# A graph attention layer: the edge and mask products of two neighbouring pairs issued together on the two halves of the array, and a new order of the stages in a round

## The chip, the cores and the metric

The kernel runs on one core of one Trainium2 chip. The metric is device time in microseconds (us), lower is better. Five engines matter: TensorE (PE, with its weight loads shown as PEld) multiplies matrices, VectorE (DVE) and ScalarE (ACT) do elementwise work and read the products out of PSUM, GpSimd (POOL) issues the gathers, and SyncE (SP) issues the other DMAs. Each engine takes its instructions in the order in which the program wrote them and waits for the others through semaphores.

## What is computed

A graph with 12,500 nodes and 400,000 edges, sorted by destination. After a layer norm and a ReLU, a GATv2 attention layer with 8 heads of 16 channels gathers over the edges, and a feed-forward block follows. The part that fills the time is the loop over edges:

```python
x_l = (x @ W_l).reshape(n, H, C)
x_r = (x @ W_r).reshape(n, H, C)
e = (ea @ W_e).reshape(-1, H, C)
m = jax.nn.leaky_relu(x_l[src] + x_r[dst] + e, NEG_SLOPE)
alpha = jnp.einsum('ehc,hc->eh', m, att)
amax = jax.ops.segment_max(alpha, dst, num_segments=n)
expa = jnp.exp(alpha - amax[dst])
denom = jax.ops.segment_sum(expa, dst, num_segments=n)
a = expa / (denom[dst] + 1e-16)
out = jax.ops.segment_sum(x_l[src] * a[:, :, None], dst, num_segments=n)
...
h = x + _gatv2(_ln(x, ln1_g, ln1_b), edge_index, edge_attr, ...)
ff = jax.nn.gelu(_ln(h, ln2_g, ln2_b) @ W1 + b1, approximate=False) @ W2 + b2
return h + ff
```

## The kernel before

A first part normalises the nodes, writes the left features to `xl_dram` and prepares the indices. Then `window_edges` works through the edges. 512 edges are a **pair** (two units of 256 edges, four tiles of 128), so there are 782 pairs, `c = 0 .. 781`. All rows are float32 except the masks.

One pair passes through these steps. Each is a function of `window_edges`, with the engine that does it:

- `gather` (POOL, L912): four indirect DMAs bring the source rows of the four tiles into `xs`, four rounds ahead. `windows` (SP, L926 to L945) brings edge attributes (`ea`), relative destinations (`dl`) and a 32-row window of right features (`zw`).
- `place` (DVE, L953): writes the 0/1 matrix of the destinations into the rows of `ea` below the 32 attribute rows, so that one product with 64 rows (32 attributes and 32 window nodes) adds the edge term and the right feature. For even pairs it also writes the mask `ne` of this pair and the next one (L959).
- `combine` (PE): four transposes of `xs` open the PSUM bank `z` (L966), and the 64-row product of `zw` and `ea` closes it (L970). A float32 product is two PE instructions in the trace. Even pairs keep their 64 rows on partitions 0 to 63 (`half`), odd pairs on 64 to 127.
- `slope` (ACT, L984) and `bend` (DVE, L989): 0.2 z, and the maximum with z, which is the leaky ReLU `m`.
- `apart` (PE, L977): a bfloat16 product of 64 rows opens the bank `ab` with a huge number for edges that do not belong to a node of the window. It uses `other`, the half of the partitions that the pair's own `zw` and `ea` do not use. `score` (PE, L994) adds the negative attention scores.
- `lowest` (DVE, L1000): the minimum over the edges of a unit, into `rec`. `weigh` (ACT, L1011, two instructions): the exponentials `p`.
- `turn` (PE, L1019): four transposes of `p` into `pt_ps`. `keep_turned` (ACT, L1024) copies them to `pt`.
- `collect` (PE, L1033): eight products add the weighted source rows into `acc`. `own_heads` (DVE, L1042 and L1048) keeps each head's own part, in `rec`, and `put` (SP, L1059) stores the record.

PSUM has four rings of two banks each: `z`, `ab`, `pt_ps` and `acc`. The work on finished groups of nodes (the `f_` functions: 25 groups of four tiles), on right features (`xr_steps`) and on some late left features (`raw_steps`) takes banks from the same rings, and is written after the stages of a round; `f_out` takes a bank of `ab`.

The order is written by hand. In round `r`, a table of stages is gone through from top to bottom, and an entry `(late, f)` does `f(r - late)`. So an engine's own order within a round is the order of the table, and `late` says by how many rounds a step follows `combine` of the same pair. Before the change a round on PE is: transposes and 64-row product of pair r, mask product of pair r-2, transposes of p of pair r-4, sums of pair r-6, scores of pair r-2. On DVE it is: own heads of r-7, lowest of r-3, bend of r-1, place of r+1. On ACT: copy of r-5, slope of r-1, exponentials of r-3.

Of the kernel before, what the change touches and what calls it, by code (L numbers as in the profile page):

```python
# [13 lines left out]
F32 = mybir.dt.float32  # L14
# [4 lines left out]
OP = mybir.AluOpType  # L19
# [3 lines left out]
P = 128  # L23
H = 8
C = P // H
DE = 32
# [811 lines left out]
def window_edges(  # L838
# [9 lines left out]
    nc = tc.nc  # L848
    SP = mybir.EngineType.SP
    KP = UP * KU  # L850
    EPR = UP * U
    LATE = 6
# [4 lines left out]
    n_pr = -(-NE // KP)  # L857
    pairs = [{} for _ in range(n_pr)]
# [7 lines left out]
    def edges_of(c):  # L866
        return [len(t) * P for t in tiles_of(c)]

    with ExitStack() as es:
# [4 lines left out]
        ps2 = es.enter_context(tc.tile_pool(name="e_ps2", bufs=2, space=PSUM))  # L874
# [74 lines left out]
        def place(c):  # L949

            d = pairs[c]
            rs = slice(d["half"].start + DE, d["half"].stop)
            nc.vector.tensor_scalar(  # L953
                d["ea"][rs].rearrange("p (a b) -> p a b", b=OW),
                d["dl"][rs].rearrange("p (a b) -> p a b", b=OS)[:, :, 0:OW],
                nid[rs], None, op0=OP.is_equal,
            )
            if c % 2 == 0:
                nc.vector.tensor_scalar(d["ne"][0 : P - DE], d["dl"][0 : P - DE, 0:EPR], nid[0 : P - DE], None, op0=OP.is_equal)  # L959

        def combine(c):

            d, e = pairs[c], sum(edges_of(c))
            z = ps2.tile([P, EPR], F32, name="z")
            for j in range(e // P):
                nc.tensor.matmul(  # L966
                    z[:, j * P : (j + 1) * P], d["xs"][:, j, 0:P], ident, start=(j == 0), stop=False, is_transpose=True
                )
            rs = d["half"]
            nc.tensor.matmul(z[:, :e], d["zw"][rs], d["ea"][rs, :e], start=False, stop=True)  # L970
            d["z"] = z

        def apart(c):
            d, e = pairs[c], sum(edges_of(c))
            d["ab"] = ps2.tile([P, EPR], F32, name="ab")
            rs = d["other"]
            nc.tensor.matmul(  # L977
                d["ab"][:, :e], farw.rearrange("p n h -> p (n h)")[rs], d["ne"][rs, :e], start=True, stop=False
            )

        def slope(c):
            d, e = pairs[c], sum(edges_of(c))
# [118 lines left out]
        def bank_of(d, name, ring="acc"):  # L1101
            d[name] = ps2.tile([P, EPR], F32, name=ring)
            return d[name]
# [99 lines left out]

        def f_out(d):
            n = d["n"]
            d["sum"] = bank_of(d, "sum", "ab")[:, 0 : n * P]
            part_out(d, 0, d["sum"])
            o = tiles("o", d, "f_e").rearrange("p t f -> p (t f)")
            part_out(d, 1, o)
            nc.vector.tensor_add(d["sum"], d["sum"], o)  # L1210
            d["o2"] = tiles("o2", d, "f_a").rearrange("p t f -> p (t f)")
            part_out(d, 2, d["o2"])
# [114 lines left out]
        def f_put(d):  # L1327
            nc.sync.dma_start(out_t[:, d["ts"], :], d["out"])

        stages = (  # L1330
            (-AHEAD, gather),
            (LATE + 1, own_heads),
            (5, keep_turned),
            (0, combine),
            (2, apart),
            (4, turn),
            (LATE, collect),
            (2, score),
            (3, lowest),
            (1, slope),  # L1340
            (1, bend),
            (3, weigh),
            (-1, place),
        )
        late_stages = (
            (-WAHEAD, windows),
# [111 lines left out]
        with tc.manual_schedule():  # L1458
            for r in range(-AHEAD, max(last_round, groups[-1]["round"] + 18)):
                in_round(r, early, groups[:-2])  # L1460
                for late, f in stages:
                    c = r - late
                    if 0 <= c < n_pr:
                        f(c)
                for late, f in sum_stages:
                    i, off = divmod(r - late, SUM_STEP)
# [9 lines left out]
                for late, f in late_stages:  # L1476
                    c = r - late
# [356 lines left out]
```

## Time and profile before

| | us |
|---|---|
| median of 3 runs (4754.81 to 4765.8) | 4760.2 |
| the profiled execution, its own time | 4798.77 |
| its span, first to last instruction | 4796.9 |
| PE busy in the span | 3841.3 (80%) |
| DVE busy | 2973.2 (62%) |
| POOL busy | 2965.3 (62%) |
| ACT busy | 2171.5 (45%) |
| mean granted PE clock | 0.897 of full |

Busy times are sums over one execution. Groups of instructions carry the line of the program, the names of what they write and read, and their shape; `64*128` behind a PE instruction is the part of the array that it uses, 64 rows by 128 columns. In a timeline, the first number is the start in us from the start of the span, the second the time that the merged instructions cover, and the bracket the idle time of the engine before them with what ended it. Ends of PE instructions are modelled, so their starts are the safer numbers. A wait that the trace ends with "remote" or "issue" has no releaser that it can name.

### The profile page before, as it was taken

The page shows a single profiled execution, that of the slowest core. Times are in us where ns is not written, and L with a number is a line of the kernel's source. Part 1 is how long each engine was busy: PE and PEld are TensorE (multiplying, and loading weights), DVE is VectorE, ACT ScalarE, POOL GpSimd, SP SyncE. Part 2 cuts the span into 40 slices and gives each one's busy share as a digit, 9 for nine tenths or more (in the row PEclk, how much of TensorE's full clock was granted, in tenths as well). Part 3 has the DMA queues.
Part 4 walks back from the last instruction along what each step waited for, and adds up shares of the span by engine and source line. Part 5 has one row for each costly group of instructions (what it writes and reads, how often), then busy time and mean ns, then how long its engine had stood idle before and what let it go on. Part 6 is the DMA issues. An engine that isn't in the chain of part 4 may idle for free.

```text
span 4796.9 us, 63161 instructions
## 1 busy us (share of the span) xinstructions
PE 3841.3 (80%) x18434; PEld 2388.1 (50%) x18435; DVE 2973.2 (62%) x6282; ACT 2171.5 (45%) x4746; POOL 2965.3 (62%) x3146
## 2 busy tenths in 40 slices
PE   2468888888888888887888888888888888888887
PEld 1335555555455555555555555555555555555554
DVE  3646676676666566566666566666666656656656
ACT  3624344344444445445444444444444454444444
POOL 6456666666666666666666666666666666666662
PEclk9679899898999999998999998899899999899898
DMA  6546666555544444444444444444444444444432
GB/s 156 173 112 149 156 158 150 138 133 132 130 99 95 92 94 96 87 85 89 93 90 92 96 94 92 84 95 82 93 97 91 92 89 87 92 87 83 94 79 66
DMA packets 625309, 502.69 MB, mean 105 GB/s; under 512 B 320174, under 2 KB 522013, under 8 KB 624717
## 3 DMA queue, kind: packets, MB, share of 16 engines
q1 hardware_dynamic: 524381, 281.11, 25.2%
q0 software_dynamic: 100000, 217.32, 21.5%
q8 instruction: 152, 2.49, 0.2%
q14 instruction: 200, 1.64, 0.1%
q10 hardware_dynamic: 576, 0.13, 0.0%
HBM read 432.27 MB, written 65.83 MB: 104 GB/s over the span
## 4 chain that ended last, share of the span: by engine, by line
PE 61%; DVE 12%; issue 11%; another core or an unknown queue 8%; ACT 2%; DMA 1%; POOL 1%; SPq 0%; DVEq 0%; ACTq 0%; POOLq 0%
PE acc L1033 15%; PE ab L994 13%; PE z L970 13%; PE pt_ps L1019 9%; PE z L966 7%; DVE rec L1000 2%; DVE ea L953 2%; DVE m L989 2%; DVE own L1042 2%; PE acc L1283 1%; PE acc L1308 1%; POOL xs L912 1%; ACT p L1011 1%; DVE ne L959 0%
## 5 line engine op out<-in xcount | busy, mean ns | idle before, releaser
L912 POOL DMA_INDIRECT xs<-xl_dram,src_sb x3009 | 2847.0, 946 | 1694.9 <-issue 787.9
L1011 ACT ACTIVATE p<-ab,rec 128x256 f32<-128x256 f32 x1563 | 656.0, 471 | 1179.5 <-DVE rec L1000 622.5
L1033 PE MATMUL acc<-xs,pt 128*128 128x136 f32 x6250 | 1017.3, 308 | 183.6 <-issue 131.3
L1042 DVE TENSOR_TENSOR own<-acc,diag 128x272 f32<-128x272 f32 x782 | 341.3, 436 | 1297.3 <-remote 517.6
L1033 PEld LDWEIGHTS acc<-xs,pt 128*128 128x128 f32 x6250 | 907.9, 214 | 213.1 <-issue 156.3
L970 PE MATMUL z<-ea,zw 64*128 64x512 f32 x1564 | 939.4, 681 | 37.6 <-issue 14.8
L1024 ACT COPY pt<-pt_ps 128x512 f32<-128x512 f32 x782 | 456.1, 583 | 1089.0 <-remote 463.9
L994 PE MATMUL ab<-m,negrep 128*128 128x512 f32 x1564 | 902.7, 659 | 29.8 <-issue 28.5
L966 PEld LDWEIGHTS z<-ident,xs 128*128 128x128 f32 x3125 | 401.6, 151 | 716.5 <-issue 346.8
L966 PE MATMUL z<-ident,xs 128*128 128x128 f32 x3125 | 519.5, 290 | 294.2 <-issue 86.5
L1019 PEld LDWEIGHTS pt_ps<-ident,p 128*128 128x128 f32 x3125 | 358.1, 150 | 729.1 <-issue 684.0
L1019 PE MATMUL pt_ps<-ident,p 128*128 128x128 f32 x3125 | 563.8, 306 | 87.7 <-issue 72.1
L953 DVE TENSOR_SCALAR ea<-dl,nid 32x516 f32<-32x516 bf16 x782 | 582.0, 744 | 29.4 <-DMA dl<-dc_dram 4.2
L989 DVE TENSOR_TENSOR m<-z,zs 128x512 f32<-128x512 f32 x782 | 532.9, 681 | 96.7 <-issue 45.1
L1000 DVE TENSOR_REDUCE rec<-ab 128x2 f32<-128x512 f32 x781 | 533.5, 683 | 76.7 <-remote 35.6
L984 ACT ACTIVATE zs<-z 128x512 f32<-128x512 f32 x782 | 475.4, 608 | 40.4 <-DMA ea<-in_ea_t 19.7
L977 PE MATMUL ab<-ne,farw 64*128 64x512 bf16 x782 | 319.2, 408 | 98.6 <-ACT p L1011 65.4
L1048 DVE TENSOR_REDUCE rec<-own 128x34 f32<-128x272 f32 x782 | 340.9, 436 | 26.8
L970 PEld LDWEIGHTS z<-ea,zw 64*128 64x128 f32 x1564 | 245.0, 195 | 199.5 <-issue 182.2
L994 PEld LDWEIGHTS ab<-m,negrep 128*128 128x128 f32 x1564 | 278.0, 216 | 52.0 <-issue 51.5
L285 POOL DMA_INDIRECT raw<-in_x,src_raw x116 | 115.0, 992 | 68.3 <-issue 36.6
L959 DVE TENSOR_SCALAR ne<-dl,nid 96x512 bf16<-96x512 bf16 x391 | 148.7, 380 | 13.1 <-DMA dl<-du_dram 0.7
(206 smaller groups left out, 2218.0 us busy)
## 6 DMA issues: line engine op xcount, KB each, us to landing
ea<-in_ea_t SPq DMA_DIRECT2D x392, 128.0 KB
ea_s<-in_ea_t SPq DMA_DIRECT2D x98, 512.0 KB
xs<-xl_dram,src_sb POOLq DMA_INDIRECT x3009
dl<-dc_dram SPq DMA_DIRECT2D x392, 66.0 KB
state<-rec SPq DMA_DIRECT2D x1563, 9.0 KB
state<-empty SPq DMA_DIRECT2D x28, 504.0 KB
f_st<-state SPq DMA_DIRECT2D x46, 288.0 KB
dl<-du_dram SPq DMA_DIRECT2D x392, 32.0 KB
```

The costliest lines, as they stand in the source:

```text
L912: nc.gpsimd.indirect_dma_start(out=xs[:, j, :], out_offset=None, in_=xl_dram, in_offset=bass.IndirectOffsetOnAxis(ap=src_sb[:, c * KP + j ...
L953: nc.vector.tensor_scalar(d["ea"][rs].rearrange("p (a b) -> p a b", b=OW), d["dl"][rs].rearrange("p (a b) -> p a b", b=OS)[:, :, 0:OW], ni ...
L966: nc.tensor.matmul(z[:, j * P : (j + 1) * P], d["xs"][:, j, 0:P], ident, start=(j == 0), stop=False, is_transpose=True)
L970: nc.tensor.matmul(z[:, :e], d["zw"][rs], d["ea"][rs, :e], start=False, stop=True)
L984: nc.scalar.activation(d["zs"][:, :e], d["z"][:, :e], AF.Copy, scale=SLOPE)
L989: nc.vector.tensor_tensor(d["m"][:, :e], d["z"][:, :e], d["zs"][:, :e], op=OP.max)
L994: nc.tensor.matmul(d["ab"][:, :e], negrep.rearrange("p n h -> p (n h)"), d["m"][:, :e], start=False, stop=True)
L1000: nc.vector.tensor_reduce(d["rec"][:, :, CX], d["ab"].rearrange("p (u e) -> p u e", e=U), AX.X, OP.min)
L1011: nc.scalar.activation(d["p"][:, us], d["ab"][:, us], AF.Exp, bias=d["rec"][:, i, CX:SH], scale=-1.0)
L1019: nc.tensor.transpose(d["pt_ps"][:, js], d["p"][:, js], ident)
L1024: nc.scalar.copy(d["pt"][:, :e], d["pt_ps"][:, :e])
L1033: nc.tensor.matmul(d["acc"][:, i, :], d["pt"][:, j * P : (j + 1) * P], d["xs"][:, j, :], start=(j == js[0]), stop=(j == js[-1]),)
```

## The change

The 64-row products of two neighbouring pairs, which lie on opposite halves of the partitions, are written next to each other: `combine` keeps the transposes alone, and a new stage `join`, in odd rounds, issues the two products of pairs r-1 and r. `apart` likewise issues the two mask products in odd rounds, of pairs r-3 and r-2. The mask comparison for even pairs leaves `place` and becomes `far`, at the end of even rounds. `slope`, `bend` and `place` run for both pairs of two in one round: slope and bend in even rounds, place in odd rounds. `score` follows by three rounds instead of two. The table begins its PE part with `collect` and ends it with `combine` and `join`; before it began with `combine`. `f_out` takes its bank from `pt_ps` instead of `ab`.

On PE an even round is then: sums of r-6, scores of r-3, transposes of p of r-4, transposes of xs of r. An odd round is: sums of r-6, two mask products (r-3, r-2), scores of r-3, transposes of p of r-4, transposes of xs of r, two 64-row products (r-1, r).

```diff
-            if c % 2 == 0:
-                nc.vector.tensor_scalar(d["ne"][0 : P - DE], d["dl"][0 : P - DE, 0:EPR], nid[0 : P - DE], None, op0=OP.is_equal)
+
+        def far(c):
+            d = pairs[c]
+            nc.vector.tensor_scalar(d["ne"][0 : P - DE], d["dl"][0 : P - DE, 0:EPR], nid[0 : P - DE], None, op0=OP.is_equal)
 
         def combine(c):
...
-            rs = d["half"]
-            nc.tensor.matmul(z[:, :e], d["zw"][rs], d["ea"][rs, :e], start=False, stop=True)
             d["z"] = z
 
+        def two(c):
+
+            return (c - 1, c) if c % 2 else (c,) if c == n_pr - 1 else ()
+
+        def join(c):
+
+            for i in two(c):
+                d, e, rs = pairs[i], sum(edges_of(i)), pairs[i]["half"]
+                nc.tensor.matmul(d["z"][:, :e], d["zw"][rs], d["ea"][rs, :e], start=False, stop=True)
+
         def apart(c):
-            d, e = pairs[c], sum(edges_of(c))
-            d["ab"] = ps2.tile([P, EPR], F32, name="ab")
-            rs = d["other"]
-            nc.tensor.matmul(
-                d["ab"][:, :e], farw.rearrange("p n h -> p (n h)")[rs], d["ne"][rs, :e], start=True, stop=False
-            )
+
+            for i in two(c):
+                pairs[i]["ab"] = ps2.tile([P, EPR], F32, name="ab")
+            for i in two(c):
+                d, e, rs = pairs[i], sum(edges_of(i)), pairs[i]["other"]
+                nc.tensor.matmul(
+                    d["ab"][:, :e], farw.rearrange("p n h -> p (n h)")[rs], d["ne"][rs, :e], start=True, stop=False
+                )
...
-            d["sum"] = bank_of(d, "sum", "ab")[:, 0 : n * P]
+            d["sum"] = bank_of(d, "sum", "pt_ps")[:, 0 : n * P]
...
+        def only(which):
+            return lambda f: lambda c: f(c) if which(c) else None
+
+        even, odd = only(lambda c: c % 2 == 0), only(lambda c: c % 2 == 1)
+        last_only, but_last = only(lambda c: c == n_pr - 1), only(lambda c: c < n_pr - 1)
         stages = (
             (-AHEAD, gather),
             (LATE + 1, own_heads),
             (5, keep_turned),
+            (LATE, collect),
+            (2, apart),
+            (2, last_only(score)),
+            (3, but_last(score)),
+            (4, turn),
+            (2, even(slope)),
+            (1, odd(slope)),
+            (2, even(bend)),
+            (1, odd(bend)),
             (0, combine),
-            (2, apart),
-            (4, turn),
-            (LATE, collect),
-            (2, score),
+            (0, join),
+            (-1, even(place)),
+            (-2, odd(place)),
             (3, lowest),
-            (1, slope),
-            (1, bend),
             (3, weigh),
-            (-1, place),
+            (0, even(far)),
         )
```

## The prediction, made before the changed kernel ran

> **What bounds the kernel now.** I read the page first: busy times, then the chain that ended last.
>
> ```profile
> PE 3841.3 (80%) x18434; PEld 2388.1 (50%) x18435; DVE 2973.2 (62%) x6282; ACT 2171.5 (45%) x4746; POOL 2965.3 (62%) x3146
> ...
> PE 61%; DVE 12%; issue 11%; another core or an unknown queue 8%; ACT 2%; DMA 1%; POOL 1%; SPq 0%; DVEq 0%; ACTq 0%; POOLq 0%
> PE acc L1033 15%; PE ab L994 13%; PE z L970 13%; PE pt_ps L1019 9%; PE z L966 7%; DVE rec L1000 2%; DVE ea L953 2%; DVE m L989 2%; DVE own L1042 2%; PE acc L1283 1%; PE acc L1308 1%; POOL xs L912 1%; ACT p L1011 1%; DVE ne L959 0%
> ```
>
> PE holds 61% of the chain, and the 64-row product (L970) 13%; the mask product (L977) is not on it. The other 39% is waiting and other engines. Next I read one round on PE in its timeline, where nothing stops it.
>
> ```profile
> 2284.57 0.60 PE L966 MATMUL z<-ident,xs 128*128 128x128 f32 x4
> 2285.10 0.69 PE L970 MATMUL z<-ea,zw 64*128 64x512 f32 x1
> 2285.11 0.39 PE L977 MATMUL ab<-ne,farw 64*128 64x512 bf16 x1
> 2285.63 0.59 PE L970 MATMUL z<-ea,zw 64*128 64x512 f32 x1
> 2286.15 0.66 PE L1019 MATMUL pt_ps<-ident,p 128*128 128x128 f32 x4
> 2286.65 1.09 PE L1033 MATMUL acc<-xs,pt 128*128 128x136 f32 x8
> 2287.58 1.02 PE L994 MATMUL ab<-m,negrep 128*128 128x512 f32 x2
> 2288.43 0.60 PE L966 MATMUL z<-ident,xs 128*128 128x128 f32 x4
> ```
>
> A round is 3.86 us at the full clock (2288.43 - 2284.57). The mask product, on the other half, starts 0.01 us after the first part of the 64-row product and is over before its second part, so two halves do work side by side, and L977 costs nothing today. But rounds last (4759 - 225) / 782 = 5.8 us on average (the first start of L989 to its last), so 1.9 us of each are something else. The granted clock, 0.897, explains 0.4 us (3.86 / 0.897 = 4.30), the work on finished groups a little. Most of the rest shows in the timeline of three engines and in the list of waits.
>
> ```profile
> 2424.09 0.66 PE L1019 MATMUL pt_ps<-ident,p 128*128 128x128 f32 x4
> 2424.59 1.09 PE L1033 MATMUL acc<-xs,pt 128*128 128x136 f32 x8
> ...
> 2431.88 0.59 ACT L1024 COPY pt<-pt_ps 128x512 f32<-128x512 f32 x1 [5.80 <-remote]
> 2431.97 0.44 DVE L1042 TENSOR_TENSOR own<-acc,diag 128x272 f32<-128x272 f32 x1 [4.92 <-remote]
> 2432.21 0.95 POOL L912 DMA_INDIRECT xs<-xl_dram,src_sb  x1 [2.15 <-remote]
> 2432.51 1.11 PE L1019 MATMUL pt_ps<-ident,p 128*128 128x128 f32 x4 [4.05 <-issue]
> 2432.80 0.68 DVE L1000 TENSOR_REDUCE rec<-ab 128x2 f32<-128x512 f32 x1
> 2433.40 0.68 DVE L989 TENSOR_TENSOR m<-z,zs 128x512 f32<-128x512 f32 x1
> ```
>
> ```profile
> POOL xs L912 <- issue: 787.9, 2573, 1.2
> DVE own L1042 <- remote: 517.6, 131, 5.8
> ACT pt L1024 <- remote: 463.9, 104, 14.6
> DVE own L1042 <- PE pt_ps L1019: 267.7, 71, 5.9
> ```
>
> ACT copies at 2431.88 what PE had transposed at 2424.09, and DVE reads at 2431.97 the sums of 2424.59; both sat idle and began within 0.1 us of each other. PE's results become known 5 to 7 us late, several at once, and meanwhile PE runs on until it needs an answer: idle 4.05 us. Two more such moments follow at 2443.87 and 2455.78, so a cycle of two rounds takes 11.9 us where PE has 7.7 us of work. In the fast stretch the copy starts at once. I do not know the cause; what matters is how far PE can run without an answer.
>
> **The change, term by term, for two rounds at the full clock.**
>
> *Removed:* two 64-row products become one block. Such a block costs 0.09 (the gap from the last transpose to the first part is 0.20, between transposes 0.11) + 0.53 + 0.52 = 1.15 us. Two blocks were 2.30; side by side they are 1.15, if the second pair's parts go as the mask product goes today, 0.01 us behind. Nearest row: L977 beside L970. Upper bound of the cost: only one part in the shadow, so three parts, 0.09 + 0.53 + 0.53 + 0.52 = 1.67. I take 1.15, since the trace shows a later instruction starting on the other half ahead of the second part.
>
> *Added:* the mask products lose their cover. Two of them side by side: 0.09 to enter, half of one float32 part (0.43 by the spacing of L994's two) = 0.21, 0.09 to leave: 0.40 us. Upper bound, one after the other at the busy time of a row: 2 x 0.39 + 0.18 = 0.96; lower bound 0.21. I take 0.40.
>
> *Sum:* 2 x 3.86 = 7.72 becomes 7.72 - 1.15 + 0.40 = 6.97 us; 0.375 us per round less. 782 x 0.375 = 293 us, over the clock 0.897: 327 us. No instruction, byte or DMA is added: `far`, `place`, `slope` and `bend` are the same instructions in other rounds. `place` of an odd pair comes one round earlier, and the DMA it needs is issued with that of the even pair three rounds ahead (the wait for `dl` before L953 is 29.4 us in 782 on the page, part of it that DMA); SP's queue keeps its order, POOL's too. The mask comparison now stands behind `lowest` in even rounds and has three rounds until its product: nothing, and 0.35 us a pair if that cover were gone. `f_out` moves 25 waits from one ring of banks to another: nothing, bound -20 to +50 us (a bank held up to two waits of a microsecond in 25 groups).
>
> *What passes through:* the saving counts where PE sets the pace, 61%: 0.61 x 327 = 200 us. Against it stand tighter returns. (a) The bank of z: in even rounds `combine` needs `bend` of the pair whose product ended the round before. Way there: 0.6 until known + slope 0.6 + bend 0.68 = 1.9 us; PE has sums 0.93 + scores 0.86 + transposes 0.44 = 2.2 us in between. It just fits; before there was a whole round. (b) The second bank of ab in odd rounds needs `weigh` of the scores of the even round: DVE does both bends first (slopes 1.2, bend to 1.9, then `lowest` 0.68, `weigh` 0.84: 0.6 + 3.4 = 4.0 us after the join), PE arrives after 0.52 + 2.67 + 0.93 = 4.1 us. Fits with nothing to spare. What waits behind a late `apart` is PE's whole queue: scores, transposes and the join, and then slope, bend and `lowest`. In the late cycles neither fits. I charge 50 us: 0.5 us (worked out below) in a quarter of the 391 cycles. Net 200 - 50 = 150 us. The profiled time, 4798.77, would become 4649; the runs shown are 0.8% below it, so median 4760 - 150 = **4610 us**, chance 0.40.
>
> The Trainium skill speaks against the first term: in "TensorE: Matmul & The Clock Gate", Part 3, matmuls start and end in strict program order, and only weight loads go ahead. By it the second pair's first part would wait for the first pair's second, which is the upper bound of 1.67. The trace does not agree: L977, written after L970, starts before L970's second part, at 2285.11 against 2285.63.
>
> **Rivals.**
>
> 1. *The returns decide: slower.* Mechanism: in even rounds the chain join, two slopes, two bends, `lowest`, `weigh`, second `apart` closes on itself every two rounds. Its length is L (until PE's result is known) + 3.4 + PE's 0.3 + 0.86 + 0.44 + 0.53 + 1.05 = L + 6.6. Before, the loop was score, L, own heads to bend 2.2 (2443.87 to 2446.03), and one round 3.86: L + 6.1; 11.9 gives L = 5.8. With that L the cycle becomes 12.4: 0.5 us in 391 cycles = +196 us: 4955. It sets the pace from L = 0.4 on (6.97 - 6.6) and costs time from L = 1.1 on, where it passes the old 7.72. For it: the 131 and 71 long waits above. Against: L shrinks when PE runs dry sooner, and the fast stretch has the copy at once. Chance 0.36.
> 2. *All of it passes:* 4760 - 327 = 4433; PE's shorter work also shortens the wait of the others. For it: 80% busy PE. Against: POOL's four gathers take 4 x 1.25 = 5.0 us a round (0.946 each and 0.30 of issue), close under 5.8. Chance 0.10.
> 3. *The halves take turns:* 1.67 instead of 1.15 leaves 0.23 us for two rounds, 391 x 0.23 / 0.897 = 100 us, of which 61% less the 50 charged is 11: 4750. Chance 0.07.
> 4. *The clock takes it back:* shorter work leaves longer gaps; if the granted clock fell from 0.897 to 0.85, PE's 782 x 3.49 = 2730 us would stretch by 2730 x (1/0.85 - 1/0.897) = 168 us, over the net 150: 4778. For it: the slices with 8 in PEclk. Chance 0.07.
>
> **How the numbers follow.** Faster by over 0.2% (what this measurement can tell from none): the forecast 0.40, the second 0.10, and 0.05 of the third and fourth: 0.55. Slower: the first, and 0.03 of the fourth: 0.39. Within 0.2%: 0.06. The range reaches from the second rival to the first, 4430 to 4960; the forecast's own, with 0.45 to 0.8 of the saving passing and the charge 0 to 100, is 4500 to 4715.
>
> **What would show it.** Right: L970's two pairs start within 0.02 us of each other, two L977 likewise, undisturbed cycles near 7.0 us for two rounds, PE's share of the chain below 61%. Wrong: L977 or the transposes L966 waiting for ACT p L1011 or DVE m L989 for hundreds of us (rival 1; now 65 and 30); L970's starts 0.53 apart, one by one (3); a clock below 0.88 (4).

## The result, and the profile after

| | before | after |
|---|---|---|
| median, us | 4759.86 | 4875.08 (4869.36 to 4882.67) |
| ratio, 95% interval | | 1.0243 [1.0222, 1.0263] |
| the profiled execution, us | 4798.77 | 4869.36 |
| its span, us | 4796.9 | 4867.6 |
| granted PE clock | 0.897 | 0.886 |

The change makes the kernel 2.4% slower; 150 us faster was forecast. These are the lines of the page of after that answer to those shown of before: the busy times, the chain by engine and by line, and POOL's gathers.

```profile
PE 3640.2 (75%) x18434; PEld 2373.2 (49%) x18435; DVE 2972.2 (61%) x6282; ACT 2152.0 (44%) x4746; POOL 2966.4 (61%) x3146
...
PE 44%; issue 20%; DVE 15%; ACT 12%; another core or an unknown queue 4%; SPq 1%; DMA 0%; ACTq 0%; DVEq 0%
PE acc L1045 12%; PE ab L1006 11%; PE pt_ps L1031 5%; PE z L981 5%; PE z L968 5%; ACT p L1023 4%; DVE m L1001 3%; DVE rec L1012 3%; PE ab L989 2%; ACT zs L996 2%; ACT pt L1036 2%; DVE ea L953 1%; DVE own L1054 1%; PE acc L1320 1%
...
L912 POOL DMA_INDIRECT xs<-xl_dram,src_sb x3009 | 2848.3, 947 | 1752.2 <-issue 795.2
```

The line of POOL's gathers on the page of before, which the reasons need too:

```profile
L912 POOL DMA_INDIRECT xs<-xl_dram,src_sb x3009 | 2847.0, 946 | 1694.9 <-issue 787.9
```

PE works 201 us less (3841.3 before), as the change means to, and its share of the chain drops from 61% to 44%. "issue", DVE and ACT take that share over. The next lines are one stretch of PE's timeline in after where nothing stops it (start, length, line, operation; x4 is four instructions in one group).

```profile
2305.61 0.39 PE L989 MATMUL ab<-ne,farw 64*128 64x512 bf16 x2
2305.93 1.12 PE L1006 MATMUL ab<-m,negrep 128*128 128x512 f32 x2
2306.89 0.60 PE L1031 MATMUL pt_ps<-ident,p 128*128 128x128 f32 x4
2307.33 0.60 PE L968 MATMUL z<-ident,xs 128*128 128x128 f32 x4
2307.86 1.13 PE L981 MATMUL z<-ea,zw 64*128 64x512 f32 x4
```

The four parts of two pairs' 64-row products (L981) take 1.13 us together; they start at 0, 0.007, 0.533 and 0.540 us. The two mask products (L989) take 0.39 us together. Such undisturbed cycles of two rounds last 7.07 to 7.10 us, where they lasted 7.73 before. But the mean cycle grew from 11.62 to 11.81 us (from the transposes of one even pair to those of the next). The list of PE's waits says where. Its first lines of before, then of after:

```profile
PE acc L1033 <- issue: 131.3, 168, 3.1
PE z L966 <- issue: 86.5, 55, 20.8
PE z L966 <- remote: 80.0, 25, 3.8
PE z L966 <- PE ab L994: 73.2, 67, 2.1
```

```profile
engine line waited for: us in total, times, longest us
PE z L968 <- issue: 287.0, 149, 8.9
PE z L968 <- DVE m L1001: 120.2, 56, 5.6
PE acc L1045 <- issue: 86.3, 73, 4.3
PE acc L1045 <- DVE own L1054: 69.2, 43, 5.9
PE ab L989 <- ACT p L1023: 68.3, 47, 4.0
PE acc L1045 <- DVE f_m L1164: 47.5, 20, 4.8
```

PE waits ahead of the transposes of xs (L968) and ahead of the sums (L1045). The next table has the same numbers for several kernels, worked out from the trace's PE records after the first 300 us of the span: the time in which a PE instruction runs, and the idle time, split by the step that comes after it. `combine` counts, for before and x8, the 64-row product too, which is part of it there (before 247 us ahead of the transposes and 36 ahead of the product, x8 20 and 51); for the others it is the transposes alone. `turn` counts also the few transposes of node features into the same ring of banks. The last six kernels are made further down; those with x have no gathers in the loop.

| kernel | ratio to before | PE runs | PE idle | ahead of `combine` | `collect` | `turn` | `apart` |
|---|---|---|---|---|---|---|---|
| before | 1 | 3736 | 755 | 283 | 184 | 91 | 99 |
| after | 1.0243 | 3530 | 1032 | 468 | 337 | 71 | 99 |
| e7_loose | 1.0249 | 3591 | 1036 | 31 | 466 | 34 | 433 |
| e8_sums_last | 1.0214 | 3484 | 1121 | 174 | 64 | 760 | 13 |
| x8_plain_before | 0.7737 | 3259 | 157 | 71 | 1 | 3 | 58 |
| x9_plain_after | 0.8507 | 3210 | 575 | 259 | 234 | 35 | 13 |
| x7_loose_plain | 0.8467 | 3250 | 514 | 69 | 289 | 39 | 74 |
| x10_sums_last_plain | 0.7687 | 3036 | 351 | 21 | 24 | 218 | 18 |

From before to after PE runs 206 us less and idles 277 us more: 71 us, and the spans differ by 70.7. So the gain was had and more than given back in waits. (The medians differ by 115 us: the profiled execution of before was 0.8% above its other runs, so the two traces show 71 of the 115.)

The list leaves many waits at "issue" or "remote", but the trace tells what ended them. A bank of `z` is free for the transposes of a pair when `bend` of the pair two before has read it. All 241 waits of over 0.15 us ahead of the transposes in after (464 us) ended 0.05 to 0.10 us after the end of just that `bend`; in before 161 of 164 did (227 of 229 us). Of the 191 waits ahead of the sums in after (329 us), 187 ended at most 0.15 us after a read of a bank of `acc`: 200 us after reads of finished groups, 126 us after `own_heads` of the pair just before, whose bank the sums need only if another user took a bank in between. So both waits are for banks. The experiments ask what sets their length, and whether the time comes back when they go.

### The profile page after: what moved, and what is told of

It reads as the page before. It is cut to its first block, busy times and chain, and to the rows that moved or that the text cites. A ratio compares the mean times of both kernels' runs of the same rounds, so it can differ in the third digit from the quotient of the medians.

```text
span 4867.6 us, 64168 instructions
## 1 busy us (share of the span) xinstructions
PE 3640.2 (75%) x18434; PEld 2373.2 (49%) x18435; DVE 2972.2 (61%) x6282; ACT 2152.0 (44%) x4746; POOL 2966.4 (61%) x3146
## 4 chain that ended last, share of the span: by engine, by line
PE 44%; issue 20%; DVE 15%; ACT 12%; another core or an unknown queue 4%; SPq 1%; DMA 0%; ACTq 0%; DVEq 0%
PE acc L1045 12%; PE ab L1006 11%; PE pt_ps L1031 5%; PE z L981 5%; PE z L968 5%; ACT p L1023 4%; DVE m L1001 3%; DVE rec L1012 3%; PE ab L989 2%; ACT zs L996 2%; ACT pt L1036 2%; DVE ea L953 1%; DVE own L1054 1%; PE acc L1320 1%
## 5 line engine op out<-in xcount | busy, mean ns | idle before, releaser
L1045 PE MATMUL acc<-xs,pt 128*128 128x136 f32 x6250 | 1031.1, 314 | 341.5 <-issue 86.3
L1045 PEld LDWEIGHTS acc<-xs,pt 128*128 128x128 f32 x6250 | 901.5, 215 | 620.6 <-issue 483.2
L1001 DVE TENSOR_TENSOR m<-z,zs 128x512 f32<-128x512 f32 x782 | 509.1, 686 | 923.1 <-ACT zs L996 588.3
L1006 PE MATMUL ab<-m,negrep 128*128 128x512 f32 x1564 | 961.0, 699 | 6.6 <-issue 6.3
L968 PE MATMUL z<-ident,xs 128*128 128x128 f32 x3125 | 535.7, 298 | 496.7 <-issue 287.0
L1031 PEld LDWEIGHTS pt_ps<-ident,p 128*128 128x128 f32 x3125 | 422.4, 153 | 591.5 <-issue 493.2
L968 PEld LDWEIGHTS z<-ident,xs 128*128 128x128 f32 x3125 | 395.9, 154 | 560.2 <-issue 338.4
L996 ACT ACTIVATE zs<-z 128x512 f32<-128x512 f32 x782 | 435.2, 605 | 316.8 <-remote 118.2
L1031 PE MATMUL pt_ps<-ident,p 128*128 128x128 f32 x3125 | 518.3, 291 | 75.0 <-issue 31.3
L981 PE MATMUL z<-ea,zw 64*128 64x512 f32 x1564 | 456.6, 657 | 0.8 <-DMA ea<-in_ea_t 0.4
L989 PE MATMUL ab<-ne,farw 64*128 64x512 bf16 x782 | 229.1, 460 | 108.7 <-ACT p L1023 68.3
L981 PEld LDWEIGHTS z<-ea,zw 64*128 64x128 f32 x1564 | 123.1, 191 | 73.3 <-issue 70.9
```

Of the source, the lines that this page charges most:

```text
L968: nc.tensor.matmul(z[:, j * P : (j + 1) * P], d["xs"][:, j, 0:P], ident, start=(j == 0), stop=False, is_transpose=True)
L981: nc.tensor.matmul(d["z"][:, :e], d["zw"][rs], d["ea"][rs, :e], start=False, stop=True)
L996: nc.scalar.activation(d["zs"][:, :e], d["z"][:, :e], AF.Copy, scale=SLOPE)
L1001: nc.vector.tensor_tensor(d["m"][:, :e], d["z"][:, :e], d["zs"][:, :e], op=OP.max)
L1006: nc.tensor.matmul(d["ab"][:, :e], negrep.rearrange("p n h -> p (n h)"), d["m"][:, :e], start=False, stop=True)
L1031: nc.tensor.transpose(d["pt_ps"][:, js], d["p"][:, js], ident)
```

## Experiments

### Four other orders on PE

Four theories: the banks of `z` are needed too early (A), the second bank of `ab` (B), rounds that begin with sums (C), the clock (D). The first kernel moves the join and the odd pair's transposes to the start of odd rounds:

```diff
+            (0, odd(combine)),
+            (0, join),
             (LATE, collect),
...
-            (0, combine),
-            (0, join),
+            (0, even(combine)),
```

> The changed kernel with one thing moved: in odd rounds the transposes and the two 64-row products stand at the start of the round instead of at its end (even rounds stay as changed). Between the end of the two products and the transposes that need the freed bank of z, PE then has 4.8 us of other work instead of 2.2, and between the scores of an even round and the second mask product 3.4 us instead of 1.8. Theory A (the bank of z comes back too late, PE waits at the transposes L968: 496.7 us in the changed kernel, 294.2 before): that wait falls to 300 us or less and the time from 4875 to 4600 to 4700. Theory C (rounds that begin with the sums meet the bank of acc too early: wait before the sums 341.5 us against 183.6): only odd rounds gain a cover, so about half of 158 us, 4800. Theory D (the clock, 0.886 against 0.897, some 40 us): no change to speak of, 4850 to 4880.

Measured, beside a before of 4745.69 us for this and the next three: 4888.6 us, 1.0291 [1.0271, 1.0311]. PE's idle time is 1040 us, 487 of it still ahead of the transposes.

The second gives each pair its mask product alone, right before its scores:

```diff
-            (2, apart),
+            (2, last_only(apart)),
+            (3, but_last(apart)),
```

> The changed kernel with the mask products apart again: each is issued alone, just before the scores of its own pair, one in every round, so that its bank of ab has been free for a round. The pairing of the 64-row products stays. By the working of the prediction PE then has 0.38 us more for two rounds (0.78 instead of 0.40), some 150 us over the loop. Theory B (the second bank of ab comes back too late): the wait before the mask products (108.7 us) goes to nearly nothing, and with it later waits: 4875 or less. Theory A or C: the time grows by the added work, 4900 to 5030.

Measured: 4854.68 us, 1.0233 [1.0216, 1.0251], clock 0.899. The wait ahead of `apart` went from 99 to 8 us and the time is the same as after's. Theory B's time (4875 or less) is met, but beside its own before nothing is gained: PE idles 114 us less than in after (918) and runs 80 us more (3610).

The third is the first with the sums behind the scores (`collect` three entries further down in the table of stages):

> As e1_join_early, and besides the sums (collect) stand behind the scores in every round, so that no round begins with them. Theory C: the wait before the sums falls by some 80 us against e1_join_early and the time with it, to some 80 us under that run. Theory A: as e1_join_early, within 30 us.

Measured: 4883.6 us, 1.0282 [1.0265, 1.0300]. The idle time ahead of the sums fell to 225 us (318 in e1), that ahead of `turn` rose to 277, and the time stayed within 5 us of e1's, not 80 below it.

In the fourth all rounds begin with transposes, and both slopes and bends stand in odd rounds:

```diff
+            (0, combine),
+            (0, join),
             (LATE, collect),
...
-            (2, even(slope)),
-            (1, odd(slope)),
-            (2, even(bend)),
-            (1, odd(bend)),
-            (0, combine),
-            (0, join),
+            (1, even(slope)),
+            (0, odd(slope)),
+            (1, even(bend)),
+            (0, odd(bend)),
```

> The changed kernel with every round beginning with the transposes, as before the change, and the two 64-row products right behind them in odd rounds; slope and bend of both pairs follow in the same odd round. PE has 2.6 us between the products and the transposes that need the bank of z, little more than the 2.2 us of the changed kernel, but no round begins with the sums. Theory C: 158 us less than the changed kernel, 4720. Theory A: the wait at the transposes stays near 500 us and the time within 60 us of 4875.

Measured: 5137.86 us, 1.0829 [1.0810, 1.0849]; PE idle 1225 us. The transposes wait for 70 us only, but the sums for 508 and `turn` for over 400.

None of the four theories holds by itself here. Three quite different orders give 1.023 to 1.029: where one wait goes, another comes. So something besides PE's order seemed to set the pace. One candidate was in POOL's rows: each gather takes 0.95 us and 0.30 of issue, so a pair takes 5.0 us, and in before the copy of `pt` starts a median 5.0 us after PE's transposes have ended (340 copies ahead of which ACT stood idle).

### The gathers taken away

The next kernels leave out the gathering by source: a plain transfer on SP's queue brings other rows instead. Their result is not the layer's; they serve for the time alone.

```diff
-            for t in tiles_of(c):
-                for j in t:
-                    nc.gpsimd.indirect_dma_start(
-                        out=xs[:, j, :],
...
+            n = sum(len(t) for t in tiles_of(c))
+            k = (c * KP) % (NT - KP)
+            nc.sync.dma_start(xs[:, 0:n, :], xl_t[:, k : k + n, :])
```

> The kernel before, with the four indirect gathers of each pair on POOL replaced by one plain transfer of four consecutive tiles on SP's queue: the gathering by src is left out, so xs holds other rows, and all other work is the same. Theory P (POOL paces the loop: a gather costs it 1.25 us with its issue, they go in bursts of eight or four, and what PE has finished is told only some 1.8 us after a burst's last gather, so two rounds take 8 x 1.25 + 1.9 = 11.9 us whatever PE does): PE's answers come at once, two rounds fall towards the undisturbed 7.73 us, so 782 rounds take 3020 to 3400 us with the granted clock, and with the 310 us around the loop the kernel takes 3350 to 3900 us. Rival R (the ring of xs, or the order of PE's waits, sets the pace and POOL is only seen waiting for it): the freeing of xs comes no earlier, and the time stays within 100 us of 4746. Rival S (SP, which now issues 782 transfers more, or the transfers' landing decides): 4500 to 5000.

> The kernel after, with the same replacement: no indirect gathers in the loop, xs holds other rows. Theory P: PE is the bound here, and then the 64-row products side by side are worth what the cycle without waits says, 7.73 - 7.07 = 0.66 us in two rounds or 391 rounds x 0.66 = 258 us, over the clock 200 to 300 us: faster than x1_plain_before by 5 to 8%, at 3100 to 3650 us. Rival R (the returns inside the changed order cost more than they save, with or without POOL): still 2% slower than x1_plain_before. Rival D (the clock gives the gain back): within 1% of x1_plain_before, with a granted clock lower by 0.03 or more.

Two more on the same chip: half of the gathers left, and memsets in their place (`for j in range(8): nc.gpsimd.memset(xs, float(j))` ahead of the plain transfer).

> The kernel before with two of each pair's four gathers left on POOL and the other two tiles taken by one plain transfer (half of the gathering by src is left out). Theory P: POOL issues 2 x 1.25 = 2.5 us a round. With one burst for two rounds, 4 x 1.25 + 1.9 = 6.9 us, less than PE's own 7.73, so PE becomes the bound and the time falls to that of x1_plain_before plus what single delays cost, 3450 to 4100 us. If the delay were a fixed 4 to 5 us in each answer whatever POOL's load: 4300 to 4746. Rival R: no change from 4746.

> As x1_plain_before (the gathering by src is left out), but POOL writes each xs tile eight times with a memset before the plain transfer fills it, some 8 x 0.55 = 4.4 us of POOL work a round that has no DMA. If any work of POOL holds back what PE tells the other engines: the time is near that of the kernel before, 4500 to 4900 us, with the same answers 5 to 7 us late. If it is the indirect gathers (POOL preparing their descriptors): the answers are prompt and the time is near that of x1_plain_before, at most 4.4 us x 782 = 3440 us of POOL plus 310, so 3350 to 3950 us.

This chip ran before in 3979.83 us, 16 to 17% less than the chips of the other runs (4746 to 4807). Measured, as ratios to it: x1 0.9246 [0.9231, 0.9262] (3681.84 us), x2 1.0151 [1.0134, 1.0168] (4041.41), x3 0.9244 [0.9229, 0.9260] (3677.36), x4 0.9774 [0.9757, 0.9790] (3889.91).

The first half of theory P came true: without gathers, or with half of them, PE's answers are prompt, and x1 is faster. The second half, that after would then win, fell: x2 is 9.8% slower than x1 (4041.41 / 3681.84). Both were repeated on a chip of the slow kind:

> x1_plain_before again (the gathering by src is left out), for the pair on one chip: 3680 us within 1% whatever this chip makes of before, if it is the gathers that make chips differ; 4200 or more on a chip where before takes 4750, if chips differ in something else.

> x2_plain_after again (the gathering by src is left out): 4040 us within 1%, and 9 to 10.5% behind x8_plain_before, if the changed order costs this with prompt answers on any chip; within 3% of x8_plain_before if the loss there was the chip's.

Measured beside a before of 4807.44 us: x8 0.7737 [0.7724, 0.7750] (3720.69 us), x9 0.8507 [0.8487, 0.8527] (4093.08). So the gathers, against plain transfers, cost before 1087 us here and 298 us on the other chip, while the kernels without them differ by 1.1 and 1.3% between the chips. And the loss of after against before is 10.0% here (4093.08 / 3720.69), 9.8% there. In the timeline of x8_plain_before an answer is prompt:

```profile
2418.29 0.66 PE L1014 MATMUL pt_ps<-ident,p 128*128 128x128 f32 x4
...
2418.79 1.09 PE L1028 MATMUL acc<-xs,pt 128*128 128x136 f32 x8
...
2418.99 0.59 ACT L1019 COPY pt<-pt_ps 128x512 f32<-128x512 f32 x1 [2.29 <-PE pt_ps L1014]
```

The transposes end at 2418.95 and the idle ACT copies at 2418.99, 0.04 us later; that is the median of all 334 such copies.

### The order on DVE and ACT

With prompt answers DVE waited 584 us for `zs` in x2, 134 in x1, since the bends stand ahead of `lowest` and the slopes behind `weigh` of the round before (theory Q). Two kernels spread the slopes and bends again:

```diff
-            (2, even(slope)),
-            (1, odd(slope)),
-            (2, even(bend)),
-            (1, odd(bend)),
+            (2, but_last(slope)),
+            (1, last_only(slope)),
+            (2, but_last(bend)),
+            (1, last_only(bend)),
```

The second, e6_bend_later, has only the two lines of `bend` of this. They ran with after itself:

> The kernel after, unchanged, beside before on this chip. Two earlier chips ran before in 4746 and 3980 us, so how late PE's answers are differs by chip. Theory Q (the changed order itself closes a chain over ACT and DVE: lowest of the odd round 0.69, weigh 0.84, keep_turned 0.58, slope 0.6, two bends 1.3, lowest of the even round 0.69, weigh 0.84, mask product 0.4, scores 1.0 us: 6.9 us and the hops, against PE's 7.07, with own heads, place and the finishing of groups besides): slower than before on any chip, 1.02 where before takes some 4750 us, 1.03 to 1.10 where it takes some 4000. Theory P (bursts of gathers on POOL decide the sign): 0.93 to 0.98 on a chip where before takes some 4000 us.

> The kernel after with one part undone: slope and bend of both pairs two rounds after their combine, so that each round has one slope and one bend, as in before, not two in even rounds. All else as in after. Theory Q: the chain over ACT and DVE is cut, DVE's waits for zs fall (x2_plain_after had 584 us, x1_plain_before 134), the kernel is 3 to 8% faster than after_again and at 0.94 to 1.00 of before. Theory P: within 0.5% of after_again. Rival Z (the bank of z: combine of an odd pair now needs the bend of the same round): waits of the transposes for DVE m grow to over 300 us and the time is that of after_again or above.

> The kernel after with only the bend of odd pairs moved to the odd round; both slopes stay in the even round. Theory Q: one bend, 0.68 us, leaves the even round's chain, 391 x 0.68 = 266 us at most: 1 to 5% faster than after_again, at or behind e5_spread. Theory P: within 0.5% of after_again. Rival Z: as after_again, with more waits of the transposes.

> e5_spread with the gathers replaced as in x2_plain_after (the gathering by src is left out). Theory Q: with one slope and one bend a round, PE is the bound again and the side by side products show: 5% or more below x2_plain_after's ratio of 1.015, down to 0.88 to 0.93 if this is a chip where before takes some 4000 us, and below 0.80 where it takes some 4750. Rival A (collect stands first in a round and waits for the sums' bank, which own heads and the finishing of groups free late): within 3% of x2_plain_after's 4041 us.

Measured beside a before of 4752.27 us: after_again 1.0254 [1.0219, 1.0288] (4868.31 us), e5 1.0172 [1.0136, 1.0208] (4842.93), e6 1.0180 [1.0158, 1.0202] (4836.33), x5 0.8918 [0.8896, 0.8941] (4245.31). Undoing "both maxima in even rounds" gives back 0.5 to 0.8%, not the 3 to 8% of theory Q. Without gathers it is slower than x2 and x9 (4041 and 4093 us): PE's idle time ahead of the transposes rises to 405 us, since the bank of `z` now comes free later. That is rival Z of e5's expectation. DVE's wait for `zs` rose too, to 815 us.

The next kernel undoes the order on DVE and ACT as a whole: `lowest` ahead of the even pair's bend, the odd pair's bend a round later, and both transposes right before their join.

```diff
-            (2, even(bend)),
-            (1, odd(bend)),
-            (0, combine),
+            (2, odd(but_last(bend))),
+            (1, odd(last_only(bend))),
+            (1, even(but_last(combine))),
+            (0, even(last_only(combine))),
+            (0, odd(combine)),
             (0, join),
-            (-1, even(place)),
-            (-2, odd(place)),
+            (-1, place),
+            (0, even(far)),
             (3, lowest),
+            (2, even(bend)),
             (3, weigh),
-            (0, even(far)),
```

> The kernel after with PE's products side by side as they are, but DVE's and ACT's order undone: lowest stands ahead of the even pair's bend, the odd pair's bend comes a round later, place of odd pairs is back in the even round, and both combines of two pairs stand right before their join, so that a bank of z has a round or more until it is needed. Theory Q2 (in after lowest stands behind the bends, these behind the slopes, these behind the weigh of the round before, and that behind its lowest, so DVE and ACT wait for each other): the waits of DVE for zs fall below 250 us (588 in e5_spread) and the time falls below after, by 2 to 6%, to 0.96 to 1.00 of before. Theory P (with late answers the order of DVE and ACT doesn't matter): 1.01 to 1.03 of before, as after_again.

> e7_loose with the gathers replaced by plain transfers (the gathering by src is left out). Theory Q2: the closed chain is gone, DVE's waits for zs fall below 150 us (584 in x2_plain_after, 815 in x5_spread_plain), PE is the bound again and the 0.66 us that two rounds save show: 2 to 7% faster than x8_plain_before, 3430 to 3620 us. Rival A (collect, first in a round, waits for the sums' bank that own heads and the finishing of groups free late, 230 us of PE's waits in x2_plain_after): the waits of L1040 stay above 150 us and the time is 0 to 6% above x8_plain_before. Rival Z (waits for z's banks): 4000 or more.

Measured, on the chip of x8 and x9: e7 1.0249 [1.0232, 1.0266] (4928.58 us), x7 0.8467 [0.8452, 0.8483] (4070.87). DVE's wait for `zs` fell to 41 us as expected, the time hardly. So that wait was a symptom, and theory Q falls. The table above shows what stayed: idle time ahead of the transposes is down from 259 to 69 us (x8 has 20), but 289 us are left ahead of the sums, which is rival A, and 74 ahead of the mask products. With the gathers, e7 has its largest new wait ahead of the mask products, 433 us.

### Both banks

PE's idle time is 157 us in x8 and 575 in x9; of the 418 between them, 188 stand ahead of `combine` (ahead of its transposes alone x8 has 20 and x9 259) and 233 ahead of the sums. The list of PE's waits in x9 names part of the holders:

```profile
PE z L963 <- issue: 164.4, 72, 4.3
PE acc L1040 <- DVE own L1049: 68.3, 58, 4.3
PE z L963 <- DVE m L996: 60.9, 46, 3.8
PE acc L1040 <- DVE f_o L1207: 42.7, 19, 4.6
PE acc L1040 <- DVE f_m L1159: 41.7, 25, 3.6
```

All 172 waits ahead of the transposes, those at "issue" too, ended 0.05 to 0.10 us after `bend` of the pair two before, and all were of even pairs. One of them:

```profile
3014.46 1.13 PE L976 MATMUL z<-ea,zw 64*128 64x512 f32 x4
...
3014.80 0.84 ACT L1018 ACTIVATE p<-ab,rec 128x256 f32<-128x256 f32 x2 [5.74 <-DVE rec L1007]
...
3015.66 1.28 ACT L626 ACT_TABLE_LOAD   x1
...
3016.95 0.21 ACT L626 ACTIVATE l_r<-l_r 128x4 f32<-128x4 f32 x1
...
3017.07 0.57 ACT L1031 COPY pt<-pt_ps 128x512 f32<-128x512 f32 x1
...
3017.53 1.09 ACT L991 ACTIVATE zs<-z 128x512 f32<-128x512 f32 x2
...
3018.16 1.29 DVE L996 TENSOR_TENSOR m<-z,zs 128x512 f32<-128x512 f32 x2 [2.51 <-ACT zs L991]
...
3018.96 0.63 PE L963 MATMUL z<-ident,xs 128*128 128x128 f32 x4 [0.95 <-PE pt_ps L1026]
```

The 64-row products end at 3015.59, but ACT has exponentials, work on late left features (L626) and a copy to do first, and takes up the slopes only at 3017.53. The first of the two maxima ends 0.69 us after its start, at 3018.85, and the transposes start 0.11 us later. (The bracket names a PE instruction that ended earlier.) In all 172 cases ACT went to the slope straight from other work.

A wait ahead of the sums is seen here:

```profile
3003.57 1.06 PE L1149 MATMUL acc<-ident,f_xr 128*128 128x128 f32 x8
...
3004.46 1.09 PE L1040 MATMUL acc<-xs,pt 128*128 128x136 f32 x8
...
3006.69 0.60 PE L963 MATMUL z<-ident,xs 128*128 128x128 f32 x4
...
3007.91 0.69 ACT L1157 ACTIVATE f_zs<-acc,el 128x512 f32<-128x512 f32 x1
...
3008.63 0.75 DVE L1159 SCALAR_TENSOR_TENSOR f_m<-acc,el,f_zs 128x512 f32<-128x512 f32 x1 [1.23 <-ACT f_zs L1157]
...
3009.53 1.43 PE L1040 MATMUL acc<-xs,pt 128*128 128x136 f32 x8 [2.24 <-DVE f_m L1159]
```

A finished group takes one of the two banks of `acc` at the end of a round (L1149), the sums that begin the next round take the other. The sums of the round after that need the group's bank, which DVE has read only at 3009.38. In before the sums stood last in the round but for the scores, behind the transposes, products and `turn`, and the group's bank had that much longer: PE idles 1 us ahead of its sums in all of x8. All 169 such waits of x9 ended within 0.15 us after a read of a bank of `acc`, 160 us of them after reads of finished groups, 70 after `own_heads` of the pair just before. The last order takes both waits away: odd rounds begin with both pairs' transposes and the join, the sums end every round, both slopes follow the join, both bends stand in even rounds.

```diff
+            (1, even(but_last(combine))),
+            (0, even(last_only(combine))),
+            (0, odd(combine)),
+            (0, join),
-            (LATE, collect),
             (2, apart),
             (2, last_only(score)),
             (3, but_last(score)),
             (4, turn),
-            (2, even(slope)),
-            (1, odd(slope)),
+            (LATE, collect),
+            (1, even(slope)),
+            (0, odd(slope)),
             (2, even(bend)),
             (1, odd(bend)),
-            (0, combine),
-            (0, join),
```

> After with the gathers replaced by plain transfers (the gathering by src is left out) and PE's products side by side, but odd rounds beginning with both pairs' transposes and their join, and the sums (collect) last in every round; both slopes right behind the join, both bends in the even round. Theory Z+S (the loss in x9_plain_after is two returns: z's banks, 259 us of waits before combine, and the sums' banks, 234 us before collect, since a round that begins with sums needs the bank that the round before has just filled): both waits together fall below 120 us, PE sets the pace, and the kernel takes 3500 to 3650 us, 2 to 6% faster than x8_plain_before's 3721. If one return stays open by the new order (apart behind weigh): 3700 to 3850. Rival Q2 (DVE and ACT order): 4000 or more. Rival D (the clock and the sums' and scores' longer busy time eat PE's saving): waits small, 3700 to 3800.

> The same order with the gathers as in after. Theory Z+S alone: if the returns are all, the kernel gains here as in the run without gathers and takes 0.94 to 0.99 of before. Theory P (with all four gathers PE's answers come 4 to 5 us late and POOL's bursts set the pace, so every order gives the same time; the waits move to other places): 1.00 to 1.03 of before, PE idle some 900 to 1050 us as in after (1032) and e7_loose (1036), 450 to 490 bursts.

Measured beside a before of 4803.77 us: x10 0.7687 [0.7670, 0.7704] (3691.84 us), e8 1.0214 [1.0192, 1.0236] (4910.23).

Without gathers the two waits together fell from 493 to 45 us, and the time from x9's 0.8507 to 0.7687. So without gathers the loss of 10.0% goes when the two waits go. A gain over before is not shown: x10 is 0.8% below x8 (3691.84 and 3720.69 us), but x8 ran on another chip, and the same kernel without gathers differed by 1% between chips; besides, x8 still has 58 us of waits ahead of `apart` that the move of `f_out` takes away. Undisturbed, two rounds of x10 take 6.79 us, but a new wait of 218 us stands ahead of `turn`, and the 3500 to 3650 of the expectation was missed. The list of waits of x10 names it:

```profile
PE pt_ps L1026 <- ACT p L1018: 115.2, 84, 4.6
...
PE pt_ps L1026 <- ACT pt L1031: 47.1, 42, 3.5
```

With the gathers the same order is as slow as the others, and the same line is now the largest of PE's waits:

```profile
PE pt_ps L1031 <- ACT p L1023: 360.4, 128, 12.4
PE pt_ps L1031 <- ACT pt L1036: 138.0, 45, 6.4
PE pt_ps L1031 <- issue: 134.7, 75, 15.2
```

PE idles 1121 us, 760 of it ahead of `turn`; 483 us of this ended with `weigh` of the pair whose `p` is turned, nearly all at even pairs. This order leaves PE as little as 2.1 us between an even pair's scores and its `turn`, where before leaves at least 4.9. So it loosens two returns and tightens a third. No order tried beats before, but none has all three loose: a kernel with `turn` a round later was not run.

## Why the prediction was wrong

**The work on PE was right in an undisturbed cycle.** The second pair's parts start 0.007 us behind the first's, and both pairs take 1.13 us (1.15 in the sum). The two mask products take 0.39 us (0.40). The undisturbed cycle is 7.07 us (6.97). Over the whole kernel less was saved than the sum's 327 us: PE runs 206 us less with gathers and 49 less without (3259 in x8, 3210 in x9), each time at a lower clock. The 223 us from x8 to x10 belong to another order. The sentence of the Trainium skill that was weighed there ("TensorE: Matmul & The Clock Gate", Part 3, strict program order) does not hold for two halves of the array in this trace: the second pair's first part starts 0.53 us before the first pair's second part, though it is written behind it. In which order the compiled program issues the four parts, no trace here shows.

**What was costed at nothing.** DVE waits 4.6 us for `dl` ahead of `place` after, 4.2 before. The move of `f_out` was worth more than nothing: in before and in x8 nearly all waits ahead of `apart` (95 and 58 us) ended with `weigh` of the pair just before, which holds the bank that the mask product needs only when `f_out` has taken one; after and x9 have none of these.

**The step that failed is "What passes through", and in it the charge of 50 us for the returns.** PE's idle time grew by 277 us, not 50. (That PE's running time fell by 206, near the 200 that step let through, is chance: the 200 is 61% of the saving, taken as the share that counts for the time, not the saving itself.) The working of (a) found that the bank of `z` "just fits" with 2.2 us on PE against a way of 1.9, and then charged 0.5 us in a quarter of the cycles. It counted slope and `bend` on that way and left out what else ACT does before it comes to the slope. From the end of the 64-row products to the end of the even pair's `bend`, after takes a median 3.9 us and x9, with prompt answers, 2.8; it is over 2.2 us in 316 of 384 and 250 of 380 cycles. Only undisturbed is it 1.4, and then it fits. In after, 79 of 240 times, ACT itself sat idle ahead of that slope, waiting for a late answer. So the transposes waited 257 us in x9, 1.5 us at a time in 172 of some 390 even rounds (20 us in x8), and 464 us in after (229 before).

Point (b), the second bank of `ab`, cost 7 us with prompt answers and 95 with late ones: these are the waits of x9 and after that end with `weigh` of the pair two before, of which before and x8 have none. That the table has 99 us ahead of `apart` both before and after is chance, since the waits for the bank of `f_out` went.

The prediction also left out a third return: the sums begin the round now and need a bank of `acc` that a finished group may have taken just before; 234 us against 1 with prompt answers, 337 against 184 with late ones (79 of the 184 lie among the eight products of a sum, not ahead of them).

**Rival 1 had the sign and not the place.** Its chain closes over the second `apart`, and the waits there are the 95 and 7 us just told, beside those for the banks of `z` and `acc`. The sign it named, hundreds of us of transposes waiting for `m`, came, though the list names only 120 of the 464. Its price of 196 us was 81 too high; after lost 115 us (4875.08 - 4759.86). And by its chain nothing would be lost below L = 1.1 us. At L = 0.04 us the loss is 372 us (x9 against x8), larger than with late answers: before then idles 157 us in all, and whatever the banks hold up shows in full.

**Rival 2's counter-evidence was the larger matter.** "POOL's four gathers take 5.0 us a round" was used to lower a chance, and never asked what it means for the 11.9 us cycle. x8 against before says 1087 of 4807 us. The charge of "61%" had read PE as the engine that sets the pace; with the gathers it doesn't alone: PE idles 755 us in before, and POOL's gathers with their issue fill 2847 + 788 = 3635 us of the span.

**The clock** fell from 0.897 to 0.886, and from 0.963 to 0.939 between x8 and x9, back to 0.962 in x10. x10 has the change's products and the clock of x8, so the products by themselves need not lower it; rival 4 would need that. What lowers it in x9 is not shown.

**What stays open.** Where the waits of after stand, and which reads ended them, is shown by the trace; that they are the loss is shown by runs for prompt answers only. With the gathers every order tried lies between 1.017 and 1.029 of before (e4 at 1.083 is apart). Whether late answers make every order as slow, or only these, each of which left some return tight, was not tested.

Why four gathers a pair hold PE's answers back is not settled either. x4's memsets kept POOL busy 3303 us and its answers stayed prompt (median 0.04 us), which speaks for the gathers and against POOL's work as such, but it ran on the chip where even before loses little to its gathers. If before's gathers and issues take 3635 us there too (x3's trace of that chip has 0.944 us a gather), then with the 283 us of before's trace ahead of the first and behind the last gather an estimate of 3918 comes close to the 3980 measured; no trace of before was taken on that chip. In before 151 of 283 late copies of `pt` start 1.75 to 1.96 us after the end of a gather, in after none of 54, so a fixed pause behind the gathers is not the rule. My idea that the change splits POOL's gathers into more bursts is not borne out: e8 has 438 bursts, before 425, after 478, and e8 is as slow as after.

## What to carry to other kernels

Before work is packed closer on an engine, write down for every bank of its rings who frees it and how much of that engine's work lies between its release and its next use; include the users that come only now and then, as the finished groups here. Count on the way to that release all that the engines on it do in between, not only the two steps of the pair: the way taken for 1.9 us was 2.8 in the median. And find out what sets the pace by taking the suspect out of both kernels on the same chip: with the gathers gone, a loss of 2.4% showed as 10%, with its two waits in plain sight. When a reordered kernel is no faster, look where its waits went before calling the order indifferent: e8 freed two returns and tightened a third.

## What the runs showed of the hardware

The kernel before took 3980 us on one chip and 4746 to 4807 on the others, with intervals far narrower than that; without its gathers it took 3682 and 3721. Even under one chip's number the record has 4746 for the runs e1 to e4 and 4807 for the later e7 and x7 to x9. Only ratios to a run of before taken beside mean anything here.

With four gathers a pair an idle ACT learned of PE's transposes a median 5.0 us late in before; without them, or with two (on the faster chip), 0.04 us.

Two 64-row float32 products on opposite halves of the array, each two PE instructions, start at 0, 0.007, 0.533 and 0.540 us and take 1.13 us together.
